# Causal attention to keys outside a unit: turned through DRAM in bands and by VectorE's square transposes instead of on TensorE

## The chip, the cores and the metric

The kernel runs on one core of one Trainium2 chip. The metric is the device time of one execution in microseconds (us); lower is better. Shown are the median of several executions and one execution taken by the hardware profiler, of which all views of the trace are.

## The reference, cut to what matters

Two transformer layers follow each other on x of 4 batches x 1024 tokens x 256 features, all in float32. The change lies in the first one's causal attention:

```python
xn = _layernorm(x)
q = jnp.einsum('bnd,dk->bnk', xn, Wq)
k = jnp.einsum('bnd,dk->bnk', xn, Wk)
v = jnp.einsum('bnd,dv->bnv', xn, Wv)
scores = jnp.einsum('bnk,bmk->bnm', q, k) * scale
att = jax.nn.softmax(jnp.where(causal, scores, -jnp.inf), axis=-1)
out = jnp.einsum('bnm,bmv->bnv', att, v)
out = _layer_norm(out + v, gamma, beta)
x = x + (jnp.einsum('bnv,vo->bno', out, Wfc) + bfc) + ffn(xn)
```

The second layer (gated attention in groups of 64, and 8 experts of which each token takes 2) is not changed, but for the place of two of its tiles.

## The kernel before, in words

The first layer works through 16 units `u` of 256 tokens: four batches `b`, in each four units `p` = 0 to 3 (`b, p = divmod(u, NP)`, NP = 4). P is 128, DC is 2 (256 features are two chunks of 128). A unit has two row tiles of 128 queries, `i` = 0 and 1. Being causal, unit p attends to the keys of units 0 to p of its batch, so tile i has t + 1 key blocks of 128, t = 2p + i.

Wq and Wk are folded into one matrix and Wv is applied after the weighting, so keys and values are both the normalised input. For a unit the program does, in this order over two turns of the loop `for u in range(U)`:

- `first(u + 3)`: layernorm on VectorE into `xn` (tokens on partitions), 7 buffers; from unit 3 on `strip` writes xn to DRAM (`xnd`, L428) and reads it back with four DMAs as 32-wide pieces (L432), so that VectorE's transpose of 32x32 squares (`first_turn`, L451) gives `xnT` (features on partitions).
- `queries` (L472) and `scores` (L488): the scores of a tile in PSUM, softmax with VectorE's causal add, maximum and scale (L490, L492, L498) and ScalarE's Exp (L495), into a tile `att` (queries on partitions, up to 1024 keys), 3 buffers.
- `turns` in the next turn of the loop: TensorE transposes each 128x128 block of att with `ident` (L522) into PSUM, up to 4 blocks to a bank; ScalarE (i = 0) or VectorE (i = 1) copies them to `attT` (L524). Parts of `hidden` (the feed-forward's first product, L509) lie between the two.
- `queries(u + 1)`, then `norms_turn(u - 1)`, which transposes the last unit's result `xl` (from `norms`, L580) on TensorE (L595), then `weighted(u)` (L533): z = att x xn with attT as the moving operand, over all key blocks j, with the xn of all units of the batch up to this one as weights; VectorE adds xnT into `zT` (L536). Then `logits` (L612), `scores(u + 1)`, the rest of `hidden`, `finish` (L549, L553) and `norms`. `multiply` (L410 to L417) folds expert weights beside it.

PSUM tiles of `bank(...)` share four buffers. Plain loads and stores go through SP's (SyncE's) DMA queue, which waits for each DMA's conditions in its turn; GpSimd issues the scattering of rows (L673). The order on each engine is mostly the order of the text; an instruction whose operands are ready earlier may be placed earlier when the program is built, and `tc.issue_after(x)` places what follows behind x on its engine.

When the first layer is done, its pool of tiles is given back; the second layer's tiles for its first batch (`tmp0`, `mid0`, `late0`, `big0`, `post0`, `side0`) take the same space, and each waits for the tiles that lay there.

Of the kernel before, what the change touches and what calls it, by code (L numbers as in the profile page):

```python
# [9 lines left out]
F32 = mybir.dt.float32  # L10
# [7 lines left out]
P = 128  # L18
B, N, D = 4, 1024, 256
NT = N // P  # L20
DC = D // P
# [46 lines left out]
def block_kernel(ctx: ExitStack, tc: tile.TileContext, x, wq, wk, wv, wfc, w1, w2, wqk, wvl, wg,  # L68
                 wo, wr, ew, el, eb2, cols, rows, rope, posb, out):
    nc = tc.nc  # L70
    pers = ctx.enter_context(tc.tile_pool(name="pers", bufs=1))
    small = ctx.enter_context(tc.tile_pool(name="small", bufs=3))
    NP = NT // 2
# [97 lines left out]
    dram = ctx.enter_context(tc.tile_pool(name="dram", bufs=1, space=DRAM))  # L171
# [4 lines left out]
    xnd = dram.tile([B * NP, 2 * P, D], F32, name="xnd")  # L176
    xld = [dram.tile([P, DC, N], F32, name=f"xld{b}") for b in range(B)]
# [59 lines left out]
    with ExitStack() as l0:  # L237
# [27 lines left out]
        early = act.tile([P, 3 * D], F32, tag="att", name="early", bufs=3)  # L265
# [161 lines left out]
        def strip(u, rows):  # L427
            nc.sync.dma_start(out=xnd[u].rearrange("(i p) d -> p i d", p=P), in_=rows)  # L428
            w = strips[u] = act.tile([P, DC, 2 * P], F32, tag="strip", name="strip", bufs=2)
            src = xnd[u].rearrange("(i r) (c j a) -> j r c i a", r=32, c=DC, a=32)  # L430
            for j in range(4):
                nc.sync.dma_start(out=w[32 * j : 32 * j + 32].rearrange("r c (i a) -> r c i a", a=32), in_=src[j])  # L432


        def first(u):
            b, p = divmod(u, NP)
            xb = xs[b]
            mv = small.tile([P, 2, 2], F32, tag="mv0", name="mv")
            for i in range(2):
                first.stats = stats(xb[:, 2 * p + i, :], mv, i, "st0")  # L440
            rstd = rstd_of(mv[:, :, 1], "rstd0", 2)
            xn = xns[u] = act.tile([P, 2, D], F32, tag="xn", name="xn", bufs=7)
            for i in range(2):
                normalise(xn[:, i, :], xb[:, 2 * p + i, :], mv, rstd, i)
            if u > 2:
                strip(u, xn)
# [31 lines left out]
        def scores(u, qT):  # L478
            b, p = divmod(u, NP)
            atts = []  # L480
            for i in range(2):
# [11 lines left out]
                att = act.tile([P, N], F32, tag="att", name="att", bufs=3)  # L493
# [5 lines left out]
                atts.append(att)  # L499
            return atts  # L500

# [14 lines left out]
        def turns(u, i, atts, attT):  # L516
            t = 2 * (u % NP) + i
            for j0 in range(0, t + 1, 4):
                js = min(4, t + 1 - j0)
                pt = bank([P, 4, P], "pt")  # L520
                for j in range(js):
                    nc.tensor.transpose(pt[:, j, :], atts[i][:, ts(j0 + j, P)], ident)  # L522
                copy = nc.vector.tensor_copy if i else nc.scalar.copy
                copy(attT[:, j0 : j0 + js, ts(i, P)], pt[:, 0:js, :])  # L524

        def weighted(u, attT):
            b, p = divmod(u, NP)
            pz = bank([P, DC, 2 * P], "pz")
            last = 2 * p + 1
            for c in range(DC):  # L530
                for j in range(last + 1):
                    q0 = P if j == last else 0
                    nc.tensor.matmul(pz[:, c, q0:], xns[b * NP + j // 2][:, j % 2, ts(c, P)],  # L533
                                     attT[:, j, q0:], start=(j == 0), stop=(j == last))
            zT = act.tile([P, DC, 2 * P], F32, tag="zT", name="zT", bufs=1)
            nc.vector.tensor_tensor(zT, pz, xnTs[u], ALU.add)  # L536
            return zT
# [153 lines left out]
        for u in range(U):  # L691
# [7 lines left out]
            if u == 1:  # L699
                fold_second(raw)  # L700
# [50 lines left out]
        q = NT - 2  # L751
# [11 lines left out]
    with ExitStack() as l1:  # L763
# [316 lines left out]
        def groups(b):  # L1080
            a = at[b]
            qlT = a.qlT = mid.tile([P, N], F32, tag="qlT", name="qlT")
            kkT = mid.tile([P, T * P], F32, tag="kkT", name="kkT")
# [127 lines left out]
        with ExitStack() as ex:  # L1211
            expw = ex.enter_context(tc.tile_pool(name="expw", bufs=2, reuse_waits="tile"))
            with ExitStack() as st:
                tmp, mid, late, big, post, side = (pool(st, n) for n in ("tmp0", "mid0", "late0", "big0", "post0", "side0"))
                tb = tmp
# [13 lines left out]
        side = tmp  # L1229
# [109 lines left out]
```

## Time and profile before

| | |
|---|---|
| median of 3 executions | 1141.13 us (1140.59 to 1142.27) |
| the profiled execution, its own time | 1137.74 us |
| its span in the trace | 1136.0 us |
| TensorE (PE) busy | 1116.2 us, 98% |
| TensorE weight loads (PEld) | 877.1 us, 77% |
| VectorE (DVE) busy | 552.0 us, 49% |
| ScalarE (ACT) busy | 295.1 us, 26% |
| GpSimd (POOL) busy | 176.3 us, 16% |
| granted TensorE clock, mean | 0.999 |
| DMA | 154.89 MB, mean 136 GB/s |

Times in the trace count from the start of the span. The first layer runs from 0 to about 520 us. Matmuls are pipelined, so the duration of one (380 ns for 256 columns) is longer than the step from one to the next. In a line of groups there stand: source line, engine, operation, output<-input, shapes, count, then busy us, mean ns of one, then the engine's idle time before and what ended it. In a line of the timeline: start, duration, engine, line, operation, count of instructions run together, and in brackets idle time before it and its releaser.

### The profile page before, as it was taken

The numbers are of one execution on the slowest core, as the hardware profiler recorded it, in microseconds if no ns is written. First come the engines' busy times: TensorE is split into PE (matmuls) and PEld (weight loads), VectorE is DVE, ScalarE is ACT, GpSimd is POOL, SyncE is SP. The second block draws the span as 40 slices with busy tenths as digits, with TensorE's granted clock in tenths as the row PEclk, the third lists the DMA queues.
The fourth block names the chain that finished last, engine by engine and source line by source line (L and its number), as shares of the span: only waits on it lengthen the run. The fifth ranks groups of instructions, "written<-read, shape, count | busy, mean of one in ns | idle before, by whom it ended". The sixth has DMA issues, their size and how long they took to land. (4 is left out here: it accounts for less than half of the span.)

```text
span 1136.0 us, 15295 instructions
## 1 busy us (share of the span) xinstructions
PE 1116.2 (98%) x5224; PEld 877.1 (77%) x5224; DVE 552.0 (49%) x1519; ACT 295.1 (26%) x766; POOL 176.3 (16%) x216
## 2 busy tenths in 40 slices
PE   8999999999999999999999999999999999999997
PEld 6788888888878888874588888888888884565645
DVE  5533554436434354445773832322232325687946
ACT  3423333233333242324301111111111113122121
POOL 2300201123121113333000000000000004363410
PEclk9999999999999999999999999999999999999999
DMA  8621432235321232321457877686876732332311
GB/s 301 186 57 59 139 89 70 93 115 151 93 88 48 76 114 77 106 103 47 153 125 253 257 237 228 204 263 197 244 224 200 256 98 69 105 93 75 91 29 38
DMA packets 163553, 154.89 MB, mean 136 GB/s; under 512 B 108305, under 2 KB 135185, under 8 KB 158353
## 3 DMA queue, kind: packets, MB, share of 16 engines
q1 hardware_dynamic: 75968, 119.00, 31.6%
q10 hardware_dynamic: 81360, 18.10, 7.4%
q0 software_dynamic: 6144, 16.79, 4.4%
q8 instruction: 42, 0.69, 0.2%
q14 instruction: 39, 0.31, 0.1%
HBM read 110.73 MB, written 44.20 MB: 136 GB/s over the span
## 5 line engine op out<-in xcount | busy, mean ns | idle before, releaser
L914 PE MATMUL p<-xT,w 128*128 128x256 f32 (+1 forms) x1152 | 241.0, 368 | 0.0
L914 PEld LDWEIGHTS p<-xT,w 128*128 128x128 f32 x1152 | 209.8, 190 | 26.3
L993 POOL DMA_INDIRECT y<-yg,slot x64 | 64.9, 1015 | 488.0 <-DVE v L1073 422.5
L919 ACT ACTIVATE s<-p,w 128x256 f32<-128x256 f32 (+1 forms) x144 | 58.7, 458 | 314.1 <-PE p L914 214.4
L922 DVE SCALAR_TENSOR_TENSOR g<-p,w,s 128x256 f32<-128x256 f32 (+1 forms) x144 | 60.9, 463 | 160.9 <-PE p L914 158.5
L935 PE MATMUL py<-w,g 128*128 128x256 f32 x544 | 123.2, 379 | 0.0
L509 PE MATMUL pm<-xnT,w_s 128*128 128x256 f32 x512 | 118.5, 380 | 0.0
L549 PE MATMUL po<-w_s,hT 128*128 128x256 f32 x512 | 116.4, 380 | 0.7 <-ACT hT L512 0.7
L935 PEld LDWEIGHTS py<-w,g 128*128 128x128 f32 x544 | 103.2, 190 | 13.7
L549 PEld LDWEIGHTS po<-w_s,hT 128*128 128x128 f32 x512 | 96.9, 190 | 21.1 <-issue 7.7
L509 PEld LDWEIGHTS pm<-xnT,w_s 128*128 128x128 f32 x512 | 95.1, 191 | 11.4
L673 POOL DMA_INDIRECT xg<-xr,put x64 | 62.2, 971 | 164.4 <-ACT hT L512 64.4
L488 PE MATMUL sc<-xnT,qT 128*128 128x256 f32 (+1 forms) x320 | 65.8, 361 | 0.0
L533 PE MATMUL pz<-attT,xn 128*128 128x256 f32 (+1 forms) x320 | 65.0, 359 | 0.0
L533 PEld LDWEIGHTS pz<-attT,xn 128*128 128x128 f32 x320 | 57.2, 191 | 6.6
L1071 PE MATMUL pv<-wvl_s,xl 128*128 128x512 f32 x128 | 57.8, 598 | 2.9 <-DVE v L1073 2.6
L553 PE MATMUL pv<-vo_s,zT 128*128 128x512 f32 x128 | 60.1, 592 | 0.0
L488 PEld LDWEIGHTS sc<-xnT,qT 128*128 128x128 f32 x320 | 54.6, 191 | 5.9 <-ACT qT L475 0.2
L1189 PE MATMUL pj<-wo_s,gd 128*128 128x256 f32 x256 | 56.7, 381 | 0.9 <-DVE gd L1170 0.4
L1142 PE MATMUL pg<-xl,wg_s 128*128 128x512 f32 x128 | 57.5, 593 | 0.0
L512 ACT ACTIVATE hT<-pm,colt 128x256 f32<-128x256 f32 x128 | 52.7, 465 | 13.9 <-PE pm L509 13.6
L1189 PEld LDWEIGHTS pj<-wo_s,gd 128*128 128x128 f32 x256 | 48.2, 190 | 8.1 <-DVE o L1191 1.1
(253 smaller groups left out, 1282.9 us busy)
## 6 DMA issues: line engine op xcount, KB each, us to landing
w<-wm SPq DMA_DIRECT2D x36, 1028.0 KB, 7.3
w<-wm SPq DMA_DIRECT2D x36, 640.0 KB, 4.6
wt<-in_ew_dram SPq DMA_DIRECT2D x16, 768.0 KB, 5.7
wm<-wt SPq DMA_DIRECT2D x16, 512.0 KB, 2.8
xt<-xg ACTq DMA_DIRECT2D x128, 64.0 KB, 5.4
yg<-yt ACTq DMA_DIRECT2D x32, 256.0 KB, 5.1
wm<-wt SPq DMA_DIRECT2D x16, 256.0 KB, 2.9
out_dram<-x SPq DMA_DIRECT2D x15, 256.0 KB, 2.1
```

What stands on the lines that cost most here:

```text
L488: nc.tensor.matmul(sc[:, kp * 2 * P : kp * 2 * P + w], qT[:, c, ts(i, P)], xnTs[b * NP + kp][:, c, 0:w], start=(c == 0), stop=(c == DC - 1))
L509: nc.tensor.matmul(pm[:, j, :], w1_s[:, c, ts(2 * m2 + j, P)], xnTs[u][:, c, :], start=(c == 0), stop=(c == DC - 1))
L533: nc.tensor.matmul(pz[:, c, q0:], xns[b * NP + j // 2][:, j % 2, ts(c, P)], attT[:, j, q0:], start=(j == 0), stop=(j == last))
L549: nc.tensor.matmul(po[:, i, :], hT[:, m, ts(i, P)], w2_s[:, m, :], start=(m == 0), stop=(m == IC - 1))
L553: nc.tensor.matmul(pv, zT[:, c, ts(i, P)], vo_s[:, c, :, :], start=(c == 0), stop=(c == DC - 1))
L673: w = nc.gpsimd.indirect_dma_start(out=xg, out_offset=bass.IndirectOffsetOnAxis(ap=put[:, b * NT + t : b * NT + t + 1], axis=0), in_=xrs[b ...
L914: nc.tensor.matmul(p[:, j, :], w13[:, w0 : w0 + P], xT[:, c, :], start=(c == 0), stop=(c == DC - 1))
L919: nc.scalar.activation(s[:, j, :], p1[:, j, :], AF.Silu, bias=w13[:, EB1 + m : EB1 + m + 1])
L922: up.g = nc.vector.scalar_tensor_tensor(g[:, m, :], p3[:, j, :], w13[:, EB3 + m : EB3 + m + 1], s[:, j, :], ALU.add, ALU.mult).ins
L935: down.last = nc.tensor.matmul(py[:, k, :], g[:, m, ts(k, P)], w2[:, m * D : (m + 1) * D], start=(m == 0), stop=(m == EC - 1)).ins
L993: w = nc.gpsimd.indirect_dma_start(out=ys[b][:, t, k, :], out_offset=None, in_=yg, in_offset=bass.IndirectOffsetOnAxis(ap=slot[:, n : n + ...
L1189: nc.tensor.matmul(pj, a.gd[:, m, ts(n, P)], wo_s[:, m, :], start=(m == 0), stop=(m == HC - 1))
```

## The change

For units with p of at least 1 (but for unit 1), `far(u)`, the attention to the keys of the units before it in the batch no longer passes through TensorE's transpose. `bands` writes the first w = 256p columns of att to a DRAM tile `atd` and reads them back with four DMAs per tile in bands: partition 32j + r gets row 32i' + r's columns jw/4 to (j+1)w/4, for the four i'. VectorE's transpose then turns all 32x32 squares, two instructions per unit, into `turned`, which lies in attT. Keys thus come in the order (j, k, a), 64p j + 32 k + a; for these matmuls the batch's xn is read from DRAM into `xn2` in the same order (four DMAs per unit), and the moving operand is a view of 8 runs of 32 columns. Only the unit's own key blocks (one for i = 0, two for i = 1) are still turned by TensorE. Units 0 to 2 are now written to `xnd` as well (`keep`). xn falls from 7 buffers to 4 and strip from 2 to 1, att rises from 3 to 4, and xn2 takes 6 KB per partition. For the second layer's first batch `qlT` and `kkT` go from pool `mid0` to `post0`.

```diff
--- before.py
+++ after.py
@@ -174,6 +174,7 @@
     xg = dram.tile([E * RS, D], F32, name="xg")
     yg = dram.tile([NF * TB + NHB * HB, D], F32, name="yg")
     xnd = dram.tile([B * NP, 2 * P, D], F32, name="xnd")
+    atd = dram.tile([B * NP, 2 * P, (NP - 1) * 2 * P], F32, name="atd")
     xld = [dram.tile([P, DC, N], F32, name=f"xld{b}") for b in range(B)]
 
     def stats(src, mv, t, tag="st"):
@@ -262,7 +263,7 @@
             for _ in range(n):
                 keep_busy.last = nc.tensor.matmul(pw, idle[:, 0:P], idle, start=True, stop=True).ins
 
-        early = act.tile([P, 3 * D], F32, tag="att", name="early", bufs=3)
+        early = act.tile([P, 3 * D], F32, tag="att", name="early", bufs=4)
         nc.scalar.dma_start(out=wq_s, in_=wq)
         load_x(0, 0)
         nc.sync.dma_start(out=wk_s, in_=wk)
@@ -424,9 +425,12 @@
 
 
 
-        def strip(u, rows):
-            nc.sync.dma_start(out=xnd[u].rearrange("(i p) d -> p i d", p=P), in_=rows)
-            w = strips[u] = act.tile([P, DC, 2 * P], F32, tag="strip", name="strip", bufs=2)
+        def keep(u):
+            nc.sync.dma_start(out=xnd[u].rearrange("(i p) d -> p i d", p=P), in_=xns[u])
+
+        def strip(u):
+            keep(u)
+            w = strips[u] = act.tile([P, DC, 2 * P], F32, tag="strip", name="strip", bufs=1)
             src = xnd[u].rearrange("(i r) (c j a) -> j r c i a", r=32, c=DC, a=32)
             for j in range(4):
                 nc.sync.dma_start(out=w[32 * j : 32 * j + 32].rearrange("r c (i a) -> r c i a", a=32), in_=src[j])
@@ -439,11 +443,11 @@
             for i in range(2):
                 first.stats = stats(xb[:, 2 * p + i, :], mv, i, "st0")
             rstd = rstd_of(mv[:, :, 1], "rstd0", 2)
-            xn = xns[u] = act.tile([P, 2, D], F32, tag="xn", name="xn", bufs=7)
+            xn = xns[u] = act.tile([P, 2, D], F32, tag="xn", name="xn", bufs=4)
             for i in range(2):
                 normalise(xn[:, i, :], xb[:, 2 * p + i, :], mv, rstd, i)
             if u > 2:
-                strip(u, xn)
+                strip(u)
 
         def first_turn(u):
             if u in strips:
@@ -490,14 +494,40 @@
                 nc.vector.tensor_tensor(sc[:, ts(t, P)], sc[:, ts(t, P)], causal, ALU.add)
                 nmax = small.tile([P, 1], F32, tag="nmax", name="nmax")
                 nc.vector.tensor_reduce(nmax, sc[:, :n], AX.X, ALU.max, negate=True)
-                att = act.tile([P, N], F32, tag="att", name="att", bufs=3)
+                att = act.tile([P, N], F32, tag="att", name="att", bufs=4)
                 rsum = small.tile([P, 1], F32, tag="rsum", name="rsum")
                 nc.scalar.activation(att[:, :n], sc[:, :n], AF.Exp, bias=nmax, accum_out=rsum)
                 rinv = small.tile([P, 1], F32, tag="rinv", name="rinv")
                 nc.vector.reciprocal(rinv, rsum)
                 scores.last = nc.vector.tensor_scalar(att[:, :n], att[:, :n], rinv, None, ALU.mult).ins
                 atts.append(att)
+                if far(u):
+                    bands(u, i, att)
             return atts
+
+
+
+
+
+        def far(u):
+            return u > 1 and u % NP
+
+        def bands(u, i, att):
+            b, p = divmod(u, NP)
+            w = p * 2 * P
+            there = atd[u][ts(i, P), 0:w]
+            nc.sync.dma_start(out=there, in_=att[:, 0:w])
+            if i == 0:
+                xn2 = act.tile([P, 2 * (NP - 1), D], F32, tag="xn2", name="xn2", bufs=1)
+                src = xnd[b * NP : u].rearrange("q t d -> (q t) d").rearrange("(j c a) d -> j a c d", j=4, a=32)
+                for j in range(4):
+                    nc.sync.dma_start(out=xn2[32 * j : 32 * j + 32, 0 : 2 * p, :], in_=src[j])
+                bands.xn2, bands.got = xn2, []
+            got = act.tile([P, N], F32, tag="att", name="band", bufs=4)[:, 0:w]
+            src = there.rearrange("(i r) (j k) -> j r i k", r=32, j=4)
+            for j in range(4):
+                nc.sync.dma_start(out=got[32 * j : 32 * j + 32].rearrange("r (i k) -> r i k", i=4), in_=src[j])
+            bands.got.append(got)
 
         def hidden(u, hT, ms):
             if 0 in ms:
@@ -515,23 +545,34 @@
 
         def turns(u, i, atts, attT):
             t = 2 * (u % NP) + i
-            for j0 in range(0, t + 1, 4):
+            for j0 in (2 * (u % NP),) if far(u) else range(0, t + 1, 4):
                 js = min(4, t + 1 - j0)
                 pt = bank([P, 4, P], "pt")
                 for j in range(js):
                     nc.tensor.transpose(pt[:, j, :], atts[i][:, ts(j0 + j, P)], ident)
                 copy = nc.vector.tensor_copy if i else nc.scalar.copy
-                copy(attT[:, j0 : j0 + js, ts(i, P)], pt[:, 0:js, :])
+                turns.copy = copy(attT[:, j0 : j0 + js, ts(i, P)], pt[:, 0:js, :]).ins
 
         def weighted(u, attT):
             b, p = divmod(u, NP)
             pz = bank([P, DC, 2 * P], "pz")
             last = 2 * p + 1
+            n = 0
+            if far(u):
+                n = 2 * p
+                turned = attT[:, 0:n, :].rearrange("p j q -> p (j q)")
+                with tc.issue_after(turns.copy):
+                    for i, got in enumerate(bands.got):
+                        nc.vector.transpose(turned[:, ts(i, n * P)], got)
+                turned = turned.rearrange("p (i k r) -> p k i r", k=n, r=32)
             for c in range(DC):
-                for j in range(last + 1):
+                for j in range(n, last + 1):
                     q0 = P if j == last else 0
                     nc.tensor.matmul(pz[:, c, q0:], xns[b * NP + j // 2][:, j % 2, ts(c, P)],
-                                     attT[:, j, q0:], start=(j == 0), stop=(j == last))
+                                     attT[:, j, q0:], start=(j == n), stop=(j == last and not n))
+                for k in range(n):
+                    nc.tensor.matmul(pz[:, c, :].rearrange("p (i r) -> p i r", r=32), bands.xn2[:, k, ts(c, P)],
+                                     turned[:, k], start=False, stop=(k == n - 1))
             zT = act.tile([P, DC, 2 * P], F32, tag="zT", name="zT", bufs=1)
             nc.vector.tensor_tensor(zT, pz, xnTs[u], ALU.add)
             return zT
@@ -697,6 +738,8 @@
             if u == 0:
                 raw = second(qTs[0])
             if u == 1:
+                for k in range(3):
+                    keep(k)
                 fold_second(raw)
             hT = act.tile([P, IC, 2 * P], F32, tag="hT", name="hT", bufs=1)
             if u == 0:
@@ -1079,8 +1122,8 @@
 
         def groups(b):
             a = at[b]
-            qlT = a.qlT = mid.tile([P, N], F32, tag="qlT", name="qlT")
-            kkT = mid.tile([P, T * P], F32, tag="kkT", name="kkT")
+            qlT = a.qlT = side2.tile([P, N], F32, tag="qlT", name="qlT")
+            kkT = side2.tile([P, T * P], F32, tag="kkT", name="kkT")
             a.attnT = post.tile([P, NT, P], F32, tag="attnT", name="attnT")
             rf = a.r.rearrange("p t i d -> p t (i d)")
             for h in range(NH):
@@ -1212,7 +1255,7 @@
             expw = ex.enter_context(tc.tile_pool(name="expw", bufs=2, reuse_waits="tile"))
             with ExitStack() as st:
                 tmp, mid, late, big, post, side = (pool(st, n) for n in ("tmp0", "mid0", "late0", "big0", "post0", "side0"))
-                tb = tmp
+                tb, side2 = tmp, post
                 tokens(0)
                 gates(0, range(0, 2))
                 values(0)
@@ -1226,7 +1269,7 @@
             exp = ex.enter_context(tc.tile_pool(name="exp", bufs=2, reuse_waits="tile"))
             experts(ahead)
         late, gat, post, mid, big, tmp = (pool(l1, n) for n in ("late", "gat", "post", "mid", "big", "tmp"))
-        side = tmp
+        side, side2 = tmp, mid
         def stores(b):
             for t in range(0, NT, 2):
                 store(b, t, 2)
```

## Prediction, made before the changed kernel was run

> **What bounds the kernel now.** I read the page first: engines, and the clock in slices.
>
> ```profile
> PE 1116.2 (98%) x5224; PEld 877.1 (77%) x5224; DVE 552.0 (49%) x1519; ACT 295.1 (26%) x766; POOL 176.3 (16%) x216
> ...
> PEclk9999999999999999999999999999999999999999
> ```
>
> TensorE is never without work for long, and its clock is granted in full. Then the stretches of the first layer, where the change lies (us, then busy us and counts of PE, PEld, DVE, ACT, POOL, clock, DMA share, GB/s):
>
> ```profile
> 60.00:500.00 440.00, 437.67 (x2151) 358.40 (x2149) 198.75 (x630) 144.76 (x434) 80.04 (x75) 1.00 0.29 92
> ```
>
> PE is busy 437.67 of 440 us, VectorE 45% and the DMA engines 29%. So a TensorE instruction taken out here is worth its step, if nothing that replaces it comes late. Third, the groups of the first layer, and who waits in it:
>
> ```profile
> L522 PE MATMUL pt<-ident,att 128*128 128x128 f32 x144 | 22.2, 280 | 0.0
> ...
> L451 DVE STREAM_TRANSPOSE xnT<-strip 128x512 f32<-128x512 f32 x13 | 9.2, 704 | 1.2 <-DMA strip<-xnd 1.2
> ...
> L524 DVE COPY attT<-pt 128x256 f32<-128x256 f32 x8 | 3.3, 415 | 0.0
> ```
>
> ```profile
> PEld pm L472 <- DVE attT L524: 4.4, 7, 0.8
> ```
>
> L522 are the transposes. L451 is the way through DRAM that the kernel already uses for xn; in 13 times its square transpose waited for the DMA once. The last line is a wait of TensorE that the transposes themselves make: `queries` needs a PSUM bank that VectorE's copy of attT still holds. Fourth, the timeline of a unit with p = 3 (u = 11), around its `turns` and `weighted`:
>
> ```profile
> 351.61 0.75 DVE L498 TENSOR_SCALAR att<-att,rinv 128x1024 f32<-128x1024 f32 x1
> ...
> 365.82 1.04 PE L522 MATMUL pt<-ident,att 128*128 128x128 f32 x8
> ...
> 366.70 1.89 PE L509 MATMUL pm<-xnT,w_s 128*128 128x256 f32 x8
> ...
> 367.24 0.74 DVE L580 TENSOR_SCALAR xl<-x,mean,rstd 128x256 f32<-128x256 f32 x2
> ...
> 367.89 1.28 DVE L524 COPY attT<-pt 128x512 f32<-128x512 f32 x2
> ...
> 368.63 1.99 PE L472 MATMUL pm<-xnT,qk_s 128*128 128x256 f32 x8
> ...
> 370.90 6.66 PE L533 MATMUL pz<-attT,xn 128*128 128x256 f32 x32
> ```
>
> From the last scaled att (352.36) to the end of the attT copies (369.17) there are 16.8 us: the time that a way through DRAM has. Last, the DMAs of the existing way (KB each, us from issue to landing):
>
> ```profile
> xnd<-xn SPq DMA_DIRECT2D x13, 256.0 KB, 2.8
> strip<-xnd SPq DMA_DIRECT2D x52, 64.0 KB, 2.7
> ```
>
> **Part 1, transposes removed.** `far` holds for u = 2, 3, 5, 6, 7, 9, 10, 11, 13, 14, 15. A unit had 4p + 3 transposes and keeps 3, so 4p go: 3 units x 4 + 4 x 8 + 4 x 12 = 92. Eight of them start at 365.82 and the next group at 366.70: 0.88 / 8 = 0.110 us a step (the 280 ns of the group is pipelined duration). 92 x 0.110 = 10.1 us off TensorE, all on the path.
>
> **Part 2, the bank wait.** Eight L509 of 256 columns take 1.89 us; less the last one's 0.38, over 7, that is 0.216 a step. From 366.70 eight steps end at 368.43, and L472 starts at 368.63: 0.20 us lost. The same working gives 0.52 us with p = 2 (331.65 to 333.90) and 0.31 us at the end of u = 15 (490.55 to 492.59). Each tile now takes one bank for its turns, so the bank that `queries` takes is one that ScalarE frees early: 4 x 0.52 + 3 x 0.20 + 0.31 = 3.0 us gained. Bounds 0 and 4.9 us (the wait line, 4.4, and 0.5 of the same kind before L595).
>
> **Part 3, VectorE between attT's copy and the weighting.** Copies of i = 1 shrink to one of 128x256, 0.42 us. Behind it stand two square transposes of 256p columns; from 704 ns for 512 that is 0.35, 0.70 and 1.06 us each (704 ns is flat plus columns, so p = 1 may be a little more). VectorE's time rises by 3 x 0.70 + 4 x 1.41 + 4 x 2.11 = 16.2 us and falls by some 6.7 us of copies (684 ns for 128x512): hidden in its idle half. What counts is when `turned` is ready. `issue_after` puts the squares right behind the copy, and `weighted` first does the own blocks, 0.33 us.
> - p = 1 (u = 9, copy at 302.62): squares done at 303.7; TensorE, earlier by 0.44, reaches the band blocks at 304.45 - 0.44 + 0.33 = 304.3. No wait.
> - p = 2 (u = 10, copy at 333.16): done at 335.0; TensorE there at 336.17 - 0.87 - 0.52 + 0.33 = 335.1. No wait, and no slack.
> - p = 3 (u = 11): the copy can't start before 367.89, behind L580. Done at 367.89 + 0.42 + 2.11 = 370.4; TensorE there at 370.90 - 1.31 - 0.20 + 0.33 = 369.7. It waits 0.7 us, in three units 2.1.
> - u = 15 has no `queries` between: done at 491.85 + 2.53 = 494.4, where the old order stood at 493.08 + 0.33 = 493.4. The unit ends 1.0 us later instead of 1.6 earlier: 2.6 us lost.
> Together 4.7 us. Bounds: 0, if other matmuls are placed into the waits, and 23.5 us, the other end of the order (third rival).
>
> **Part 4, DMAs and SP's queue.** Per far unit SP gets 14 issues more (2 stores, 8 band loads, 4 for xn2); `keep` adds 3 once. At 0.38 us (xnd) and 0.63 us (strip) an issue that is 8.3 us of a turn of some 30. The store of a tile waits for L498, its loads for the store's landing, and behind them stand `strip(u + 3)`, the next stores of expert weights (L417) and loads (L397, L402). None of those is needed for half a turn. Nearest rows for u = 11: store issued 352.4, landed 355.2, four loads issued until 357.7, the last landed at 359.8; wanted at 368.3. So 8.5 us in hand. One whole strip in front (0.38 + 2.8 + 2.5 = 5.7) still fits, as do the slowest landings shown (6.2 and 6.0 us; +6.7). Cost 0; if the cover is gone, VectorE stands at the squares and every microsecond beyond 8.5 is TensorE's.
>
> **Part 5, the moving operand and the tiles.** The 92 band matmuls (4p a unit) replace as many of 256 columns, now in 8 runs of 32. No matmul of before reads in runs, so the bound is from 0 to a doubled step, 92 x 0.216 = 19.9 us; below 0 nothing, as the columns are the same. I take 0: the nearest row, L451's transposes, writes such runs at the pace of a plain 128x512 operation (704 against 684 ns). xn's 4 buffers suffice, since a unit's xn is now read by its own weighting alone (unit 1's by unit 0's too). One strip buffer is freed by `first_turn` a turn before it is refilled. `qlT` and `kkT` are first written at groups(0), some 25 us after the first layer's last reader: 0.
>
> **Sum.** -10.1 - 3.0 + 4.7 = -8.4 us: the profiled execution goes from 1137.74 to 1129.3. The median stood 3.39 us above it, so 1132.7.
>
> **Skill against trace.** L451's 704 ns for four 128x128 blocks and L522's 0.110 us a block say that TensorE's way is the cheaper per block, but on the engine that is full. The Trainium skill (VectorE: DVE Perf Modes, "The three transpose paths") gives 390 ns for a 128x128 block on TensorE, and warns that a plain DMA whose strides do the transposing is 19 times slower than the hardware's own; by its 390 ns the 92 blocks would be worth an estimated 36 us, and the warning speaks against the change. It names large strides of the innermost run as its case; here runs are 256 to 768 bytes long, and the strips, with runs of 128 bytes, land in 2.7 us.
>
> **Rivals.**
> 1. *Bands late (slower).* SP does one thing after another: a strip with slow landings in front (0.38 + 6.2 + 2.5 = 9.1 us), or a store's landing under a 768 KB load (L402, 5.7 us), takes more than the 8.5 us. For it: SP already waited 16.7 us for xnd's landings (5 times), and gets three such waits a turn. Against: L451 waited 1.2 us in all, and the DMA engines are 29% busy. It decides from 8.4 / 11 = 0.8 us of lateness a unit; at 2 us it is +22 - 8.4, 1154.7. A wait that makes TensorE idle could also cost clock, which shows 1.00 throughout here. The Trainium skill (TensorE: Matmul & The Clock Gate, "HAM oscillation") puts that at gaps over some 3.4 us; no run here shows it. 0.16.
> 2. *A draw.* The bank wait stays in another form (0 for 3.0) and the p = 2 units, without slack, lose 0.7 us each: -10.1 + 4.7 + 2.8 = -2.6, 1138.5; a little more and it is within the noise. 0.10.
> 3. *VectorE's order (slower).* If other ready work (a square transpose of xnT, 0.70, and the layernorm of two tiles, L181, L182, L211, 0.9 + 0.25 + 0.8) is placed between copy and squares, `turned` comes 2.6 us later: 8 x 2.35 = 18.8 more in units with p of 2 and 3: 1151.5. For it: these run wherever VectorE was thought idle. Against: `issue_after` and data long present. 0.09.
> 4. *Runs of 32 cost a doubled step:* 1152.6. 0.05.
>
> **How the numbers follow.** Forecast 0.60, at 1128 (Part 3 at 0) to 1138; draw 0.10; slower 0.30. A measurement here tells some 0.2%, 2.3 us: faster means below 1138.8, slower above 1143.4. The draw's time lies on the edge, and I count it as same. The likeliest case's own range is 1128 to 1138. The whole range goes up to 1149, which leaves out about half of the slower cases, and some 0.04 below. 1132.7 us; faster 0.60, same 0.10, slower 0.30.
>
> **What would show it.** L522 at 52 instead of 144; 22 square transposes more, none idle "<-DMA"; PE busy in the first layer less by some 10 us; L472 no longer waiting on L524; a wait of L533 on the squares of 0.7 us at p = 3 and over 1 us at u = 15; the step inside the band matmuls still 0.216. Wrong: idle time of VectorE or TensorE behind the band loads, or a step above 0.216.

## The result, and the profile after

| | before | after |
|---|---|---|
| median | 1140.95 us (1140.59 to 1142.27, 4 executions) | 1128.54 us (1128.31 to 1128.96, 4 executions) |
| the profiled execution | 1137.74 us, span 1136.0 | 1128.42 us, span 1126.7 |

The ratio is 0.989, with a 95% interval of 0.9877 to 0.9903: the changed kernel is faster by 12.4 us in the medians. The prediction said 1132.7 us (8.4 less), with a range of 1128 to 1149. Profile against profile it is only 9.3 us; where the other 3.1 lie is told further down.

In the changed program the lines have other numbers: L522 is now L552 (transposes), L524 is L554 (their copies), L533 is L571 (own blocks) and L574 (bands), L566 are the squares, L472 is L476, L509 is L539, L580 is L621, L595 is L636, L549 and L553 are L590 and L594.

The page's line of engines, the clock in slices, and the same stretch of the first layer as before (us, then busy us and counts of PE, PEld, DVE, ACT, POOL, clock, DMA share, GB/s):

```profile
PE 1106.9 (98%) x5132; PEld 867.4 (77%) x5132; DVE 555.4 (49%) x1533; ACT 288.7 (26%) x758; POOL 177.7 (16%) x216
...
PEclk9999999999999999999999999999999999999999
```

```profile
60.00:500.00 440.00, 439.21 (x2119) 359.08 (x2118) 214.23 (x686) 141.37 (x437) 90.02 (x83) 1.00 0.45 137
```

TensorE has 92 instructions fewer (5132 for 5224). In the stretch its idle time fell from 2.33 to 0.79 us, VectorE's work rose to 49% and the DMA share from 0.29 to 0.45. So TensorE does less and waits less. The groups:

```profile
L552 PE MATMUL pt<-ident,att 128*128 128x128 f32 x52 | 11.6, 288 | 0.0
L574 PE MATMUL pz<-attT,xn 128*128 128x256 f32 x184 | 43.8, 382 | 0.0
L566 DVE STREAM_TRANSPOSE attT<-band 128x768 f32<-128x768 f32 x8 | 7.3, 954 | 0.0
L566 DVE STREAM_TRANSPOSE attT<-band 128x512 f32<-128x512 f32 x8 | 5.2, 688 | 0.0
L554 DVE COPY attT<-pt 128x256 f32<-128x256 f32 x15 | 6.3, 417 | 0.0
```

52 transposes are left of 144. No square transpose has idle time ahead of it (the last column is 0.0), so no band was late. Who waits in 60 to 500 us, weight loads and matmuls (engine, line waited for: us, times, longest):

```profile
PEld pt L636 <- ACT hT L542: 1.2, 1, 1.2
PEld pz L574 <- DVE attT L566: 0.8, 1, 0.8
```

```profile
PE pt L636 <- DVE xl L621: 0.8, 1, 0.8
```

The wait of `queries` on the copies of attT (4.4 us, 7 times before) is gone altogether. What has come for it is one place, in unit 15. The same unit as in the prediction, u = 11, in the timeline of after:

```profile
357.63 1.89 PE L476 MATMUL pm<-xnT,qk_s 128*128 128x256 f32 x8
357.70 0.42 DVE L554 COPY attT<-pt 128x256 f32<-128x256 f32 x1
358.04 0.73 DVE L621 TENSOR_SCALAR xl<-x,mean,rstd 128x256 f32<-128x256 f32 x2
...
358.68 1.83 DVE L566 STREAM_TRANSPOSE attT<-band 128x768 f32<-128x768 f32 x2
...
359.79 0.82 PE L571 MATMUL pz<-attT,xn 128*128 128x256 f32 x4
...
360.56 2.86 PE L574 MATMUL pz<-attT,xn 128*128 128x256 f32 x12
...
363.26 0.81 PE L571 MATMUL pz<-attT,xn 128*128 128x256 f32 x4
...
363.91 2.76 PE L574 MATMUL pz<-attT,xn 128*128 128x256 f32 x12
```

`queries` runs into `weighted` without a gap. The squares are done at 360.51 (358.68 + 1.83), and TensorE begins the band blocks at 360.56, 0.77 us after its own blocks. In the second half of the unit (the other 128 features), where nothing is left to wait for, the same way takes 0.65 us (363.26 to 363.91). So TensorE does stand here for the squares, for 0.12 us, too short for the list of waits. The bands of this unit had been issued until 341.68 + 1.73 and 347.45 + 1.73 us, long before. The second run of band matmuls has (2.76 - 0.38) / 11 = 0.216 us a step, the step of the old ones; the first, right behind the squares, has (2.86 - 0.38) / 11 = 0.225, which is another 0.1 us.

**Where the time went, unit by unit.** I take for each unit the time of its last L553 (L594) matmul from the first matmul of the program, and compare how much earlier each comes than in the kernel before; the difference from one unit to the next is what that unit gained.

| units | forecast, each | measured, each | over all |
|---|---|---|---|
| p = 1 (5, 9, 13) | 0.44 | 0.44 | 1.3 |
| p = 2 (2, 6, 10, 14) | 1.40 | 1.62 | 6.5 |
| p = 3 (3, 7, 11) | 0.82 | 1.40 | 4.2 |
| 15 | -1.0 | -0.50 | -0.5 |
| 4 and 8 (p = 0) | 0 | 0.40 and 0.52 | 0.9 |
| first layer | 8.4 | | 12.4 |

(Units 0, 1 and 12 add 0.06.) The second layer, whose text is the same, gives back 3.5 us between 527 and 1005 us, 2.9 of them between 984 and 1005 us: VectorE stands there for 2.81 us ahead of one addition (L1234).

### The profile page after: what moved, and what is told of

Same layout as the page of the kernel before. It is cut to its first block, busy times and chain, and to the rows that moved or that the text cites. A ratio compares the mean times of both kernels' runs of the same rounds, so it can differ in the third digit from the quotient of the medians.

```text
span 1126.7 us, 15401 instructions
## 1 busy us (share of the span) xinstructions
PE 1106.9 (98%) x5132; PEld 867.4 (77%) x5132; DVE 555.4 (49%) x1533; ACT 288.7 (26%) x758; POOL 177.7 (16%) x216
## 5 line engine op out<-in xcount | busy, mean ns | idle before, releaser
L539 PE MATMUL pm<-xnT,w_s 128*128 128x256 f32 x512 | 118.5, 379 | 0.0
L590 PE MATMUL po<-w_s,hT 128*128 128x256 f32 x512 | 116.1, 380 | 0.0
L590 PEld LDWEIGHTS po<-w_s,hT 128*128 128x128 f32 x512 | 96.9, 190 | 20.1 <-issue 8.0
L539 PEld LDWEIGHTS pm<-xnT,w_s 128*128 128x128 f32 x512 | 95.6, 192 | 11.6
L594 PE MATMUL pv<-vo_s,zT 128*128 128x512 f32 x128 | 60.1, 592 | 0.0
L980 DVE TENSOR_TENSOR yt<-py,w 128x512 f32<-128x512 f32 (+1 forms) x36 | 23.8, 662 | 59.0 <-PE py L978 59.0
L603 DVE SCALAR_TENSOR_TENSOR x<-pv,rs,x 128x256 f32<-128x256 f32 x32 | 15.5, 484 | 72.1 <-ACT rs L189 47.7
```

Source lines behind the costliest of these rows:

```text
L539: nc.tensor.matmul(pm[:, j, :], w1_s[:, c, ts(2 * m2 + j, P)], xnTs[u][:, c, :], start=(c == 0), stop=(c == DC - 1))
L590: nc.tensor.matmul(po[:, i, :], hT[:, m, ts(i, P)], w2_s[:, m, :], start=(m == 0), stop=(m == IC - 1))
L594: nc.tensor.matmul(pv, zT[:, c, ts(i, P)], vo_s[:, c, :, :], start=(c == 0), stop=(c == DC - 1))
```

## The experiments

The theory: the gain is the 92 transposes and the bank wait, on an engine that is full; VectorE's squares fit, but for unit 15; the bands come several us ahead of need. The rivals of the result: the transposes were hidden and what helped was VectorE's changed order; or the squares and the copies are what decides. Runs 0 to 3 were made on one chip (before: 1138.16 us, 1137.81 to 1139.58), 4 to 7 on a second (before: 1138.24 us, one execution), 8 to 11 on a third (before: 1141.72 us, 1139.97 to 1142.21).

### 0. The kernel before, once more

> The kernel before, unchanged, profiled a second time. The first profile of it (1137.74 us) lies 3.2 us under the median of its runs; the changed kernel's profile (1128.42) lies on its median (1128.54), and in it VectorE stands still for 2.8 us at 989.7 with its operands long there. Theory 1: such a standstill is in most executions of the kernel before too, at another place, and the first profile happened to miss it: this profile takes about 1140.5 us and the 3 us lie in the second layer (behind 520 us), the first layer being the same within 0.3 us. Theory 2: the standstill belongs to the changed kernel, and the first profile of before is typical: this one again takes 1137 to 1138 us.

Measured: 1138.91 us. In the first layer it agrees with the first profile within 0.2 us unit by unit; at the passage to the second layer's experts it is 1.29 us later. So steps of units can be compared to better than 0.1 us, while the passage varies by about 1 us from execution to execution; and there is no standstill in that stretch of the second layer. That is theory 2 so far; runs 8 and 9 come back to it.

### 1. Unit 15 keeps TensorE's transposes

```diff
         def far(u):
-            return u > 1 and u % NP
+            return u > 1 and u % NP and u + 1 < U
```

> The changed kernel with unit 15 alone turned by TensorE again (far(u) also needs u + 1 < U). From the traces unit 15 ended 0.5 us later by the change, since no queries cover VectorE's squares there. Theory 1 (the squares' wait ate the gain of that unit): the first layer ends 0.5 us earlier than in the changed kernel (unit 15's last L594 at 501.2 instead of 501.7 us from the first matmul). Theory 2 (the 0.5 us come from something else, such as the order of other work): no earlier, or later by up to 1.3 us, the 12 transposes.

Measured: 1124.63 us (1124.42 to 1125.76), ratio 0.9881 (0.9864 to 0.9897). Unit 15's step is +0.21 us against -0.50 with the bands: the bands cost 0.71 us there. The rest of the difference to 1128.54 is not unit 15's: the standstill of the second layer is not in this profile (run 9 takes it up).

### 2. The 92 transposes again, into PSUM that nobody reads

```diff
             t = 2 * (u % NP) + i
+            for j0 in range(0, 2 * (u % NP), 4) if far(u) else ():
+                js = min(4, 2 * (u % NP) - j0)
+                pt = bank([P, 4, P], "pt")
+                for j in range(js):
+                    nc.tensor.transpose(pt[:, j, :], atts[i][:, ts(j0 + j, P)], ident)
```

> The changed kernel plus the 92 transposes that it saved, into PSUM tiles that nobody reads (no copies). Theory 1 (the gain is TensorE's 92 steps plus waits that came with the copies): +10.0 us, by unit 0.44 (p = 1), 0.87 (p = 2), 1.31 (p = 3), so still some 2.4 us ahead of before. Theory 2 (all the gain is the transposes and their banks): +12.4 us, as slow as before. Theory 3 (the gain comes from elsewhere, so that transposes would hide): under +5 us.

Measured: 1132.55 us (1132.17 to 1133.39), ratio 0.995 (0.9933 to 0.9967). The group of the added transposes is there in full (line, tile and shape, count, busy us and mean ns, idle before):

```profile
L552 PE MATMUL pt<-ident,att 128*128 128x128 f32 x92 | 14.3, 280 | 0.0
```

What each unit gains against the kernel before: -0.06 us with p = 1, +0.75 with p = 2, +0.30 with p = 3, -0.22 in unit 15; units 4 and 8 gain 0.41 and 0.51 as in the kernel after. The difference to the steps of after is the price of the transposes: 3 x 0.49 + 4 x 0.87 + 3 x 1.10 = 8.2 us for 80 of them outside unit 15, 0.103 us each, near the 0.110 of the prediction. In unit 15 they cost nothing (the unit is 0.28 us shorter with them), since they lie in its waits. That makes 8.0 us, not the 10.0 of theory 1, but well above the 5 of theory 3: the rival that the transposes were hidden falls. What is left, 0.75 and 0.30 us a unit, I put down to the bank wait: the transposes are back, but the wait of `queries` (L476) on a copy of attT is not in this profile's list of waits, so it went with the copies and not with the transposes. Run 3 brings it back.

### 3. The transposes and their copies

As run 2, and each bank is also copied to attT, which the squares then overwrite:

```diff
+                copy = nc.vector.tensor_copy if i else nc.scalar.copy
+                copy(attT[:, j0 : j0 + js, ts(i, P)], pt[:, 0:js, :])
```

> As the run with dead transposes, but their PSUM tiles are also copied to attT by ScalarE and VectorE as before, and then overwritten by the squares. All that the change removed is back, all that it added stays. Theory 1 (the copies cost TensorE a bank wait, 3.0 us in the prediction; the rest of the gain is that VectorE's order around xnT's transpose and xl became a better one): +10.0 + 2 to 3.7 us, about as slow as before, perhaps more, since VectorE now has copies and squares in one row (up to +8). Theory 2 (no bank wait was gained): the same as the run without copies, within 0.5 us.

Measured: 1143.59 us (1143.38 to 1143.85), ratio 1.0045 (1.0028 to 1.0061): 11.0 us above run 2, with copies of VectorE and ScalarE alone. With p = 3 a unit is 2.03 us longer than in run 2. Two waits of the first layer (matmuls on `hidden`, weight loads on `queries`), and VectorE at u = 11:

```profile
PE pm L539 <- DVE attT L554: 4.7, 4, 1.4
```

```profile
PEld pm L476 <- DVE attT L554: 1.5, 2, 0.8
```

```profile
369.30 0.74 DVE L628 TENSOR_SCALAR xl<-x,mean,rstd 128x256 f32<-128x256 f32 x2
369.95 1.02 DVE L554 COPY attT<-pt 128x512 f32<-128x512 f32 x2
371.21 1.83 DVE L573 STREAM_TRANSPOSE attT<-band 128x768 f32<-128x768 f32 x2
```

The squares begin behind two copies more, but they are not in TensorE's list of waits: `hidden`, and twice `queries`, wait for a bank that VectorE's copy holds. So this is not the third rival of the prediction (squares that come late), but the bank wait, larger than before the change. The run also puts back more than the change took away: a tile's own blocks now have a bank and a copy of their own, so that a tile with p = 3 needs three banks and not two, one with p = 1 two and not one, and one with p = 2 two as before. In just this way units 3, 7 and 11 (p = 3) and those with p = 1 are 1.73 and 0.34 us longer than in the kernel before, and those with p = 2 are not (0 to 0.63 us shorter). How much of the 11 us the additional bank makes is not told apart here.

### 4 and 5. The bands held up by copies from DRAM to DRAM

Two hops (run 4) and four (run 5) between the store of a tile and its band loads:

```diff
+            for h in hop:
+                nc.sync.dma_start(out=h[u][ts(i, P), 0:w], in_=there)
+                there = h[u][ts(i, P), 0:w]
             got = act.tile([P, N], F32, tag="att", name="band", bufs=4)[:, 0:w]
```

> The changed kernel with the bands' way made longer: between the store of att and the band loads the data is copied twice more from one DRAM tile to another, each waiting for the one before. With some 2.5 us for each that is 5 us later. Theory 1 (the bands lie 7 to 8 us in hand: in unit 11 the last band load is issued at 349.2 and the squares start at 358.7 us): the first layer's end moves by less than 0.5 us. Theory 2 (the slack is smaller, since what stands behind on SP's queue is late too): +1 us a unit and more, 11 us and more.

> The same with four copies more from DRAM to DRAM, some 10 us later in all. Theory 1 (slack 7 to 8 us, then every microsecond counts): VectorE waits for the band loads at the squares, 2 to 4 us a unit, +20 to +45 us; the granted clock stays at 1.0 if the waits are short. Theory 2 (other work on TensorE fills the wait, or SP's other transfers collide first): under +10, or far over +45 us.

Measured: 1156.31 us and 1239.76 us. SP's queue in run 4, with p = 3 (start, duration of the issue, line, output<-input):

```profile
381.58 0.52 SPq L528 DMA_DIRECT2D hop<-atd  x1
...
386.74 1.89 SPq L528 DMA_DIRECT2D hop<-hop  x1
...
391.72 1.81 SPq L533 DMA_DIRECT2D band<-hop  x4
```

One hop of 384 KB holds the bands up by 5 us, so two are 10 us late and not the 5 or so that I had reckoned with; the numbers under theory 1 of both expectations are missed, for that reason in part. The shape is as the slack of the prediction (8.5 us at p = 3) has it: with 10 us more, units of p = 1 lose nothing or 0.3 us against the kernel after, those of p = 2 0.3 to 0.5, those of p = 3 but unit 15 6.7 to 15.1. That is far more than the 1.5 us by which 10 exceeds the slack. In run 4 VectorE stands for band loads only twice, 2.9 us in all. The program's order was planned anew around the hops: in unit 11 the second square comes 17 us behind the first (383.59 and 400.99 us), and TensorE does other work between the own blocks and the bands. It stands 6.4 us in all at the squares, and in unit 3 the granted clock is down as well (0.50 from 122 to 126 us); the rest is not accounted for. With some 20 us more (run 5) every unit from 2 on but those with p = 0 loses, VectorE stands for the band loads, and TensorE's clock falls in slices (waits of VectorE in the first layer, then the page's clock):

```profile
DVE attT L570 <- DMA band<-hop: 29.3, 16, 4.3
```

```profile
PEclk8999899898898989998979999999999999999999
```

So the first rival of the prediction (bands late) is a true mechanism, that begins between 0 and 10 us of further lateness. In run 5 the mean clock is 0.963, with waits of TensorE of up to 5.5 us. By the Trainium skill (TensorE: Matmul & The Clock Gate, "HAM oscillation") idle gaps of TensorE beyond some 3.4 us lower its clock; run 5 agrees.

### 6. The copy of attT behind xl, in the kernel after

In the kernel after the copy stands ahead of `xl`. Here it is put behind, as it was in the unit with p = 3 before (`norms.xl` is the second of the two instructions that write xl; the line that notes it is left out here):

```diff
-                turns.copy = copy(attT[:, j0 : j0 + js, ts(i, P)], pt[:, 0:js, :]).ins
+                with tc.issue_after(norms.xl) if i and far(u) else nullcontext():
+                    turns.copy = copy(attT[:, j0 : j0 + js, ts(i, P)], pt[:, 0:js, :]).ins
```

> The changed kernel with VectorE's copy of attT (i = 1) put behind xl (L621), as the prediction had it; in the changed kernel it was placed ahead of xl. Theory 1 (that order is why units with p = 3 waited 0.2 us and not 0.7): squares end 0.4 us later, units 3, 7, 11 end 0.3 to 0.7 us later each, others unchanged, in all +1 to +2 us. Theory 2 (the order does not matter, own blocks cover it): within 0.3 us.

Measured: 1124.74 us. Units with p = 3 gain 1.34 instead of 1.40 us, all others the same to 0.06. Copy and xl both stand ahead of the squares in either order, so that at u = 11 the squares end only 0.05 us later, counted from the start of the own blocks (360.55 - 359.78 against 360.51 - 359.79). TensorE follows by as much: 0.82 us from the own blocks to the band blocks instead of 0.77. So that the copy moved ahead of `xl` is not why p = 3 came out better than forecast.

### 7. The turn of xn behind xl, in the kernel before

In the kernel before, in units 4 and 8, VectorE's transpose of a strip stands ahead of `xl`. `xl` is then turned by TensorE (L595) and copied, and `logits` (L612) waits for that (u = 8):

```profile
274.16 0.71 DVE L451 STREAM_TRANSPOSE xnT<-strip 128x512 f32<-128x512 f32 x1
274.79 0.12 DVE L573 TENSOR_TENSOR var<-var,rstd 128x2 f32<-128x2 f32 x1
274.83 0.42 DVE L524 COPY attT<-pt 128x256 f32<-128x256 f32 x1
...
275.93 0.73 DVE L580 TENSOR_SCALAR xl<-x,mean,rstd 128x256 f32<-128x256 f32 x2
...
276.74 0.60 PE L595 MATMUL pt<-ident,xl 128*128 128x128 f32 x4
...
279.02 1.11 PE L612 MATMUL pl<-wqr_s,xlT 128*128 128x72 f32 x8 [0.37 <-ACT xlT L600]
```

```diff
-                nc.vector.transpose(xnT, strips[u])
+                with tc.issue_after(norms.xl) if u > 3 else nullcontext():
+                    nc.vector.transpose(xnT, strips[u])
```

> The kernel before with one order changed: VectorE's square transpose of xnT (L451) is put behind xl of the same turn of the loop. In it, units 4 and 8 lose 0.43 and 0.53 us at logits, and there L451 stands just ahead of xl's chain; in the changed kernel it does not, and these units gained 0.40 and 0.52 us that the prediction did not have. Theory 1 (L451's place is the cause): units 4 and 8 end 0.4 and 0.5 us earlier than in before, the others the same. Theory 2 (the cause is in the change itself, in ScalarE's shorter copies or in banks): no change.

Measured: 1140.9 us against 1138.24. Units 4 and 8 gain 0.41 and 0.31 us, and with p = 3 the units lose 0.6 each. So of the 0.9 us that units 4 and 8 gained unforeseen 0.7 are this order, which the changed program happens to have too: all of it in unit 4 and 0.3 of 0.5 in unit 8. Runs 2 and 3 say the same from the other side: these units gain 0.41 and 0.51 us there too, with the transposes back. Done alone for every unit the order does not pay, but by less than the two times say: 1.71 us of the difference have arisen by the end of unit 0, which the edit does not touch. There the granted clock is down from 22 to 29 us (0.55, 0.50, 0.50 and 0.75 in stretches of 2 us from 22 on), where the first profile of before shows 1.00.

### 8. The kernel after, on a third chip

> The kernel after, unchanged, on a further chip, for two things. The ratio to the kernel before: theory and rival both 0.987 to 0.991. And the 2.8 us in which VectorE stood ahead of its addition at L1234, 37 us or so before the end of the attention of the second layer's last groups, with its operands long there: if it belongs to the placement of this kernel's instructions (rival), it stands at the same instruction in this profile too, at 1.5 to 3 us; if it is an accident of one execution (theory), no wait of over 1 us stands there, and the profile's time is 1124 to 1126 us against some 1138 of the kernel before.

Measured: 1127.97 us (1127.14 to 1128.84) against 1141.72, ratio 0.9887 (0.987 to 0.9903). The first layer's steps agree with the first profile of after within 0.01 us from unit 1 on. The standstill is there again, at the same instruction (first profile of after, then this one):

```profile
992.54 0.42 DVE L1234 TENSOR_TENSOR o<-pj,rowt 128x256 f32<-128x256 f32 x1 [2.81 <-PE pj L1232]
```

```profile
991.27 0.42 DVE L1234 TENSOR_TENSOR o<-pj,rowt 128x256 f32<-128x256 f32 x1 [2.80 <-PE pj L1232]
```

So it is not an accident of one execution, as my theory had it. The view names the matmuls of pj as what VectorE waited for; in run 6, with the same instructions up to there, the same addition follows without a wait. But it is not the kernel's either: see run 9.

### 9. Unit 15 as before, on the third chip

The kernel of run 1, once more.

> The kernel in which unit 15 keeps TensorE's transposes, again, now beside the kernel after on one chip. Theory (the last unit has no later work to hide its bands' squares and its VectorE is full, so that it loses some 0.7 us of the 12 that the other units gain): 0.3 to 1.0 us below the kernel after in the median, once neither has a standstill. Rival (the difference of the first runs, 1124.6 against 1128.5, was the standstill and a second chip alone): within 0.3 us of it.

Measured: 1127.13 us (1126.72 to 1127.58), ratio 0.9878 (0.9862 to 0.9894). The same program that had no standstill on the first chip has it here:

```profile
990.96 0.42 DVE L1234 TENSOR_TENSOR o<-pj,rowt 128x256 f32<-128x256 f32 x1 [2.81 <-PE pj L1232]
```

All four kernels profiled on the third chip lose 2.8 to 2.9 us between the same two milestones (in runs 10 and 11 in two waits at this line, of 1.5 and 1.2 us); on the other two chips none of runs 0 to 7 does. So it goes with the chip or the conditions of the run, not with the change. The kernel before is 3.5 us slower on the third chip as well, but there is no profile of it there: that it is the same standstill is not shown.

The gain of unit 15's old way is 0.84 us in the medians beside run 8; the ranges overlap, and some 0.5 us of the 0.71 that the unit gains is given back at the passage to the second layer, by the milestones of the two profiles. It is less than 0.1% below the kernel after: not told apart by this.

### 10. qlT and kkT back in the pool of before

```diff
-                tb, side2 = tmp, post
+                tb, side2 = tmp, mid
```

> qlT and kkT of the second layer's first batch go back from pool post0 to mid0, as in the kernel before; the rest as after. The prediction put the pools at 0. Theory (tiles laid out with mid0 one step larger put v of that batch over xl and xr, which scatters of the first layer read until late): v's writes wait at the passage to the second layer, 3 to 6 us longer than the kernel after. Rival (the passage is set by the gates and the experts' first loads whatever lies where): within 0.5 us of the kernel after, first layer the same within 0.2.

Measured: 1135.41 us, 7.4 us more than the kernel after on this chip. From unit 1 on the first layer is the same; 7.5 us are lost at the passage (timeline, then two stretches, in which the granted clock stands behind the five engines):

```profile
522.52 1.29 DVE L1116 TENSOR_TENSOR v<-pv,rowt 128x512 f32<-128x512 f32 x2 [7.00 <-DMA xg<-xr,put]
...
523.26 3.78 PE L1114 MATMUL pv<-wvl_s,xl 128*128 128x512 f32 x4 [5.34 <-DVE v L1116]
```

```profile
522.00:524.00 2.00, 0.74 (x1) 0.50 (x2) 1.32 (x4) 0.65 (x1) 0.00 (x0) 0.64 0.00 0
524.00:526.00 2.00, 2.00 (x4) 0.69 (x3) 0.00 (x0) 1.99 (x3) 0.00 (x0) 0.50 0.00 0
```

The first write of v waits until the last scattering of rows of `xr` has been done: v's place now overlaps `xr`, as the theory said. TensorE waits 5.34 us there, and 0.66 us at the same place in run 8: 4.7 us more, within the 3 to 6 of the theory. Behind the wait the granted clock is 0.64, 0.50, 0.50 and 0.66 in the stretches of 2 us from 522 to 530, where run 8 has 1.00; the remaining 2.8 us fit that. So the move of the two tiles is no tidying: with the new buffers of the first layer it saves 7.5 us, some 60% of what the whole change brings.

### 11. Unit 1 too

```diff
         def far(u):
-            return u > 1 and u % NP
+            return u % NP
...
             if u == 0:
+                keep(0)
                 raw = second(qTs[0])
...
-                for k in range(3):
+                for k in range(1, 3):
```

> Unit 1 too takes the bands (unit 0's xn goes to DRAM for it), the rest as after. If its bands and its xn2 come in time, it gains what the other units of p = 1 do, 0.44 us. Theory (SP's queue is full of the first loads until some 38 us, and landings take 6 to 10 us there): unit 1's band squares wait for DMA, and it ends 2 to 8 us later than in the kernel after. Rival: 0.2 to 0.6 us earlier.

Measured: 1129.83 us, 1.9 us more than run 8's median. Unit 1 gains 0.44 us, just as the other units with p = 1, so the theory of late bands falls. But unit 15 loses 1.69 us to the kernel after, and the clock shows why (stretches of unit 15, run 8 and then run 11):

```profile
482.00:484.00 2.00, 2.00 (x11) 1.77 (x10) 0.00 (x0) 0.00 (x0) 1.53 (x3) 1.00 0.36 134
484.00:486.00 2.00, 2.00 (x12) 1.79 (x11) 0.00 (x0) 0.00 (x0) 0.47 (x1) 1.00 0.20 78
```

```profile
482.00:484.00 2.00, 2.00 (x6) 1.56 (x7) 0.00 (x0) 0.00 (x0) 1.83 (x2) 0.50 0.55 197
484.00:486.00 2.00, 2.00 (x8) 1.65 (x7) 0.00 (x0) 0.00 (x0) 1.21 (x2) 0.65 0.16 66
```

The granted clock is 0.50 and 0.65 there, after the unit's two waits (0.80 us of PE at L636, 0.76 us of PEld at L574), which in runs 8 and 11 are equal to 0.01 us. One execution: whether the dip comes back is open. Another 1.42 us are lost by the end of unit 0, where the clock is down for longer than in run 8 (0.62 and 0.70 in the stretches 20 to 25 and 25 to 30 us, against 0.68 and 0.98). So the time of this run does not show that unit 1 is better left alone; the unit itself gains.

## Why the prediction was right, step by step

- **The transposes (10.1 us): right in the mechanism, 8.0 us in size.** Run 2 gives 8.2 us outside unit 15, and there -0.3. The step of 0.110 us held (0.103 measured); what was mis-sized is unit 15, where 12 transposes were counted at 1.3 us and lie in waits, and to a lesser part the units with p = 3, where 12 cost 1.10 instead of 1.31: with them in front TensorE comes to the band blocks late enough not to wait for the squares.
- **The bank wait (3.0 us): right, and too small.** In run 2 it stays away with the transposes back, so that it is the copies that hold the banks. Without the transposes' price, the units with p = 2 gain 0.75 instead of 0.52 us, those with p = 3 0.30 instead of 0.20 (run 2): 3.9 us for 2.7. I had taken one gap, that between L509 and L472, where the wait line of 4.4 us (my upper bound of 4.9) held more.
- **The wait on the squares with p = 3 (0.7 us, three times): wrong in size; it is 0.2.** TensorE stands 0.12 us there and loses 0.1 in the steps behind (see u = 11 above). Two numbers of that step were off, both the same way. "The own blocks, 0.33 us": each float32 matmul stands as two instructions in the trace (L574 x184 for 92), and the own blocks take 0.65 us (363.26 to 363.91). And two squares of 768 columns take 1.83 us, not 2.11 (954 ns each in the group, overlapping by some 0.1). That makes 0.32 + 0.28 = 0.60 us less to wait.
- **Unit 15 (lose 2.6, net -1.0): right in the mechanism, -0.50.** It is the one place where TensorE stands for the squares for longer: from the own blocks to the band blocks it is 1.80 us (479.40 to 481.20) instead of 0.65, and part of that was filled by `multiply`:

```profile
479.40 0.82 PE L571 MATMUL pz<-attT,xn 128*128 128x256 f32 x4
480.15 1.12 PE L411 MATMUL pab<-lt 16*128 16x512 f32 x2
481.20 2.46 PEld L574 LDWEIGHTS pz<-attT,xn 128*128 128x128 f32 x12 [0.76 <-DVE attT L566]
```

- **DMAs and SP's queue (0, with 8.5 us of cover at p = 3): right.** No square waited for its band. How far the cover goes is known only within bounds: nothing lost as it is, 7 to 15 us a unit with 10 us more of lateness.
- **Runs of 32 columns (0; bound a doubled step): right.** 0.216 us a step in after, as before. The bound was too low by half, since 184 instructions, and not 92, have this step: a doubled step would have been 39.7 us, and that rival at 1172 us instead of 1152.6, both outside the range.
- **Pools (0): right for the change as made,** and not because the tiles don't matter: run 10.
- **Order of VectorE in units 4 and 8 (not foreseen): 0.9 us gained,** 0.7 of it shown by run 7.
- **Sum.** 0.9 (units 4 and 8) + 0.9 (p = 2) + 1.7 (p = 3) + 0.5 (unit 15) is the 4.0 us between forecast and result. The result lies only 0.5 us above the lower end of the range, and the errors went both ways: less for the transposes, more for the banks, smaller waits at the squares, and the two units not foreseen. That the range held is in part luck. So is the step from the profile to the median, +3.39 us: the first profile of before, at 1137.74 us, fits the chips without the standstill, where before has a median of 1138.2, while its first median of 1141 fits the third chip, which has it. By that reading the two first profiles differ by the 12.4 us of the first layer, less some 3 us of standstill that only the second of them has; no profile of before with the standstill exists to confirm it.
- **Skill against trace.** The Trainium skill (VectorE: DVE Perf Modes, "The three transpose paths") gives 390 ns for one 128x128 block in bf16 on TensorE, an estimated 36 us for 92. As a price of float32 blocks one behind the other that does not fit: 0.103 us a block in run 2. The slowness of strided DMA of which it warns does not show with runs of 768 bytes: the band loads of 96 KB in run 4 landed in 2.5 us (median of 28).

## What to carry to other kernels

On an engine that is full, price a removed instruction by its step, not its duration, and then look for the waits that go with it: here the PSUM banks that the copies of the transposed blocks held were worth nearly half as much as the transposes themselves, and putting the transposes back without their copies lost 8.0 of the 12.4 us. Work moved to another engine is free only as long as what is queued there, and the banks that it holds, still fit: the same squares with the copies back beside them, in up to one bank more a tile, made the kernel slower than before. The last turn of a pipelined loop has no neighbour to hide such work, and buffers that change size move the tiles of the next stage onto others: weigh these two places by themselves.

## What the runs showed of the hardware

- On one chip VectorE stood for 2.8 us ahead of one addition (in two parts in two of the four profiles); on two others the same instructions ran without that wait (runs 0 to 7). Why is open. Profiles of two kernels should come from the same chip before differences of 3 us are read out of them.
- In run 11 the clock fell to 0.50 for some 3.4 us after two waits of under 0.9 us (0.50 and 0.65 in two stretches of 2 us), and it stayed at 1.00 after the same waits in run 8. Between 20 and 30 us, where TensorE's longest wait is 1.59 us, it falls in ten of the fourteen profiles (to 0.50 from 24 to 26 us in the first profile of after), and in the first profile of before it does not (1.00). The Trainium skill (TensorE: Matmul & The Clock Gate, "HAM oscillation") names gaps over 3.4 us; these were shorter, so its rule does not tell when a dip comes here.
- Behind a wait of 5.34 us (run 10) the clock was below 1.00 in four stretches of 2 us; of the 7.5 us lost there 4.7 are the wait.
- A copy of 384 KB from DRAM to DRAM landed in 3.8 us (median of 7), and a chain through SP's queue took 5 us for each.
- A float32 matmul stands as two instructions with a weight load each (L574: 184 and 184 for 92), a transpose as one (L552: 52); to count steps, count the trace's instructions, not those of the text.
